# Gathered products of a sparse graph layer: units of 256 rows with 64-row quarters, paired half tiles, and the identity term folded into the matrix

## The chip, the cores and the metric

The kernel runs on one core of a Trainium2 chip. The time is the device time of that core in microseconds, the median of several executions. A profile is one execution taken by the hardware profiler; it has a span of its own, from the first to the last instruction.

## The reference

One layer of a graph network with a residual and a normalisation, in float32, for a batch of 8, 4096 nodes and 256 features:

```python
HW = einsum('bnf,fo->bno', x, W)
A_norm = relu((A + A.T) * 0.5)
D = sum(A_norm, axis=1);  d = where(D > 0, D, 1) ** -0.5
L_norm = eye(N) - d[:, None] * A_norm * d[None, :]
out = relu(einsum('nm,bmo->bno', L_norm, HW))
return layernorm(x + out, axis=-1, eps=1e-5)
```

A is 4096 x 4096 and mostly zero: an entry (i, j) is present with a probability that falls with i and j, so the first rows and columns are the densest; the diagonal is always present. After symmetrising, 70,020 of 16.8 million entries are not zero (counted from the inputs of seed 0).

With e = 1/d² and g = d · HW, an output row is relu(d (e g_self − Σ A_norm g)). This is the form that the kernel computes. The dense matrix is never multiplied: for each block of output rows the kernel lists the nodes with an entry in those columns of A, gathers their rows of g and their pieces of A from device memory, and multiplies tiles of 128 gathered rows.

## The kernel before

**Stage 1** goes through A in blocks of 512 x 512 (`NS` = 8 per side). For a pair (i, j), i ≤ j, SP's queue loads both blocks (`load_adj`, L201), and `symmetrise` transposes one on PE against the identity (L212), DVE adds the other (L215), ACT applies relu and the factor 0.5 (L216), DVE sums each row over the 128-wide column blocks into `part` (L217), and ACT's queue stores the block to `a_dram` (L223). When a row i of blocks is done, `degrees` sums `part`, sets `e` (L233) and lets POOL raise it to −0.5 for `r` (L234). Between the blocks `form` makes g, 128 nodes at a time: load x (SP, L241), transpose it on PE (L247), copy to SBUF on ACT (L248), multiply by W (L257), and scale by r on ACT (L266) into `g_dram`; the last 8 blocks are formed unscaled first, held in SBUF (L268), and scaled when r is known (`release`, L276). `a_dram` and `g_dram` have one row more, N, which holds zeros.

**Lists.** For four blocks of 128 output columns at once, `places` marks in `mask` which nodes have a positive sum in a block, counts them with two matmuls (triangular and all-ones matrices, L114, L115), and turns the running count into a place (tile, row) for each node (L117 to L143). `make_list` spreads the places of one block into one-hot matrices on DVE (`hot`, L149; `inn`, L156; `val`, L163 and L166), and 32 small bf16 matmuls collect the node numbers (L169). From these DVE makes the row numbers of g and of A (`gi`, `ai`, L183, L185). A place that nobody takes gets N, the row of zeros. `CAP` gives the number of tiles of each of the 32 blocks, 29 for the first, 9 for the last nine, 390 in all. Lists are made four blocks ahead; the order of instructions on an engine is that of a scheduler's planning, so some of them run in stage 1.

**Gathered products.** For block i, `gather` issues two indirect DMAs on POOL for each tile t: 128 pieces of A of 128 columns (`ga`, L358, 64 KB) and 128 rows of g of 2048 columns (`gg`, L365, 1 MB), each into one of 10 buffers. The product of a tile is four matmul calls (L384), one for each 512 columns (8 batches x 256 features are G = 2048), which add into four PSUM banks `py`; six banks are there for them. `finish` loads x again (`xr`, L313, SP's queue) and the block's own rows of g (`gself`, L394), lets DVE compute e·gself − py (L317), ACT relu with scale r (L325), and DVE the residual sum (L326), the moments (L331 to L333) and, after POOL's power (L334), the normalisation (L336). ACT's queue stores the result (L344).

After it stands a branch for the case that a list is too long (`over`); it forms the dense product and isn't entered for these inputs.

Of the kernel before, what the change touches and what calls it, by code (L numbers as in the profile page):

```python
# [16 lines left out]
CAP = [29, 21, 18, 17, 16, 15, 14, 13, 13, 13, 12, 12, 12, 11, 11, 11, 11] + [10] * 6 + [9] * 9  # L17


@with_exitstack  # L20
def kernel(
# [20 lines left out]

    nc = tc.nc
    B, N, F = x.shape
    FO = w.shape[1]
    P = 128
# [5 lines left out]
    G = B * FO  # L52
    HOLD = 8
    EPS = 1e-5

    const = ctx.enter_context(tc.tile_pool(name="const", bufs=1))
    dram = ctx.enter_context(tc.tile_pool(name="dram", bufs=1, space=bass.MemoryType.DRAM))
    psum = ctx.enter_context(tc.tile_pool(name="psum", bufs=6, space=bass.MemoryType.PSUM))
# [5 lines left out]
    part = const.tile([P, NB, NB], F32, name="part")  # L64
# [3 lines left out]
    r = const.tile([P, NB], F32, name="r")  # L68

# [11 lines left out]
    tmax = max(CAP)  # L81
# [19 lines left out]
    carry = const.tile([P, A, NB], F32, name="carry")  # L101
    nc.vector.memset(carry, 1.0)
    nc.vector.memset(carry[:, :, 0:1], 0.0)
    over = const.tile([P, NB], F32, name="over")

    def places(s):

        mask = ipool.tile([P, A, NB], BF16, tag="mask", name=f"mask_{s}")
        nc.vector.tensor_scalar(
            mask, part[:, :, s * A : (s + 1) * A].rearrange("p m i -> p i m"), 0.0, None, ALU.is_gt  # L110
        )
        pc = psum.tile([P, 2, A * NB], F32, tag="ix", name=f"count_{s}", bufs=2)
        mflat = mask.rearrange("p i m -> p (i m)")
        nc.tensor.matmul(pc[:, 0, :], lhsT=lower, rhs=mflat, start=True, stop=True)  # L114
        nc.tensor.matmul(pc[:, 1, :], lhsT=ones, rhs=mflat, start=True, stop=True)  # L115
        incl = ipool.tile([P, A * NB], F32, tag="incl", name=f"incl_{s}")
        nc.vector.tensor_tensor_scan(  # L117
            incl, carry.rearrange("p i m -> p (i m)"), pc[:, 1, :], 0.0, ALU.mult, ALU.add
        )
        for k in range(A):  # L120
            i = s * A + k
            nc.vector.tensor_scalar(
                over[:, i : i + 1],
                incl[:, (k + 1) * NB - 1 : (k + 1) * NB],
                float(CAP[i] * P),
                None,
                ALU.is_gt,
            )
        pos = ipool.tile([P, A * NB], F32, tag="pos", name=f"pos_{s}")
        nc.vector.tensor_sub(pos, incl, pc[:, 1, :])  # L130
        nc.vector.tensor_add(pos, pos, pc[:, 0, :])
        ip = ipool.tile([P, A * NB], I32, tag="ip", name=f"ip_{s}")
        nc.vector.tensor_copy(ip, pos)
        quot = ipool.tile([P, A * NB], I32, tag="quot", name=f"quot_{s}")
        nc.vector.tensor_single_scalar(quot, ip, 7, ALU.arith_shift_right)
        rem = ipool.tile([P, A * NB], I32, tag="rem", name=f"rem_{s}")
        nc.vector.tensor_single_scalar(rem, ip, P - 1, ALU.bitwise_and)

        at = ipool.tile([P, 2, A, NB], F32, tag="at", name=f"at_{s}")
        aq = at[:, 0].rearrange("p i m -> p (i m)")  # L140
        nc.vector.scalar_tensor_tensor(aq, quot, 1.0, mflat, ALU.add, ALU.mult)
        nc.vector.tensor_scalar(aq, aq, -1.0, None, ALU.add)
        nc.vector.tensor_copy(at[:, 1].rearrange("p i m -> p (i m)"), rem)  # L143
        return at

    def make_list(i, at):
        k, t = i % A, CAP[i]
        hot = ipool.tile([P, NB, P], BF16, tag="hot", name=f"hot_{i}")
# [3 lines left out]
            at[:, 1, k, :].unsqueeze(2).to_broadcast([P, NB, P]),  # L152
            ALU.is_equal,
        )
        inn = ipool.tile([P, NB, tmax], F32, tag="inn", name=f"inn_{i}", bufs=1)
# [3 lines left out]
            at[:, 0, k, :].unsqueeze(2).to_broadcast([P, NB, t]),  # L159
            ALU.is_equal,  # L160
        )
        val = ipool.tile([P, NB, 2, tmax], BF16, tag="val", name=f"val_{i}")
# [4 lines left out]
        pl = psum.tile([P, 2, tmax], F32, tag="ix", name=f"pl_{i}", bufs=2)  # L167
        for m in range(NB):
            nc.tensor.matmul(  # L169
                pl[:, :, :t],  # L170
                lhsT=hot[:, m, :],
                rhs=val[:, m, :, :t],
                start=(m == 0),
                stop=(m == NB - 1),
            )

        low = ipool.tile([P, tmax], F32, tag="low", name=f"low_{i}")
        nc.vector.tensor_copy(low[:, :t], pl[:, 1, :t])
        nc.vector.scalar_tensor_tensor(
            low[:, :t], pl[:, 0, :t], float(P), low[:, :t], ALU.mult, ALU.add  # L180
        )
        gi = ipool.tile([P, tmax], U32, tag="gi", name=f"gi_{i}", bufs=6)
        nc.vector.tensor_scalar(gi[:, :t], low[:, :t], float(N), None, ALU.add)  # L183
        ai = ipool.tile([P, tmax], U32, tag="ai", name=f"ai_{i}", bufs=6)
        nc.vector.tensor_scalar(  # L185
            ai[:, :t], low[:, :t], float(NB), float(N * NB + i), ALU.mult, ALU.add
        )
        lists[i] = (gi, ai)


    with (
# [4 lines left out]
        tc.tile_pool(name="stat1", bufs=2) as stat1,  # L196
    ):
# [9 lines left out]
        def symmetrise(i, j, tij, tji):  # L207
            sym = spool.tile([P, A, S], F32, tag="sym", name=f"sym_{i}_{j}")
            for a in range(A):
# [8 lines left out]
                part[:, i * A : (i + 1) * A, j * A : (j + 1) * A],  # L218
                sym.rearrange("p a (c q) -> p a c q", q=P),
# [5 lines left out]
            )  # L225

        def degrees(i):
            ms = slice(i * A, (i + 1) * A)
            deg = stat1.tile([P, A], F32, tag="deg", name=f"deg_{i}")
            none = stat1.tile([P, A], F32, tag="none", name=f"none_{i}")  # L230
            nc.vector.tensor_reduce(deg, part[:, ms, :], AX.X, ALU.add)
            nc.vector.tensor_scalar(none, deg, 0.0, None, ALU.is_le)
            nc.vector.tensor_add(e[:, ms], deg, none)  # L233
            nc.gpsimd.tensor_tensor(r[:, ms], e[:, ms], neg_half[:, :A], ALU.pow)  # L234

# [46 lines left out]
        for i in range(NS):  # L282
            for j in range(i, NS):
# [14 lines left out]
            known += range(i * A, min((i + 1) * A, NB - HOLD))  # L298
        for m in sorted(held):
            release(m)  # L300
        ats = {}
        ahead = 4
        for i in range(ahead):
            if i % A == 0:
                ats[i // A] = places(i // A)
            make_list(i, ats[i // A])
# [4 lines left out]
    def finish(i, gself, py, ypool, stat):  # L311
        xr = ypool.tile([P, B, F], F32, tag="xr", name=f"xr_{i}")
        nc.sync.dma_start(xr, x[:, i * P : (i + 1) * P, :].rearrange("b p f -> p b f"))  # L313
        y = ypool.tile([P, B, FO], F32, tag="y", name=f"y_{i}")
        yf = y.rearrange("p b o -> p (b o)")
        for c in range(G // S):
            nc.vector.scalar_tensor_tensor(  # L317
                yf[:, c * S : (c + 1) * S],
                gself[:, c * S : (c + 1) * S],
                e[:, i : i + 1],  # L320
                py[c],
                ALU.mult,
                ALU.subtract,
            )
        nc.scalar.activation(yf, yf, AF.Relu, scale=r[:, i : i + 1])  # L325
# [4 lines left out]
        for b in range(B):  # L330
            nc.vector.bn_stats(stats[:, b, :], y[:, b, :])  # L331
            nc.vector.bn_aggr(mv[:, b, :], stats[:, b, :])
        nc.vector.tensor_scalar(rstd, mv[:, :, 1], EPS, None, ALU.add)  # L333
        nc.gpsimd.tensor_tensor(rstd, rstd, neg_half[:, :B], ALU.pow)  # L334
# [9 lines left out]
        nc.scalar.dma_start(out[:, i * P : (i + 1) * P, :].rearrange("b p f -> p b f"), y)  # L344

    a_rows = a_dram.rearrange("j (c q) -> (j c) q", q=P)
    with (
        tc.tile_pool(name="gath", bufs=10) as gath,
        tc.tile_pool(name="ypool", bufs=2) as ypool,
        tc.tile_pool(name="stat", bufs=3) as stat,  # L350
    ):
        got = {}

        def gather(i):
            gi, ai = lists.pop(i)
            for t in range(CAP[i]):
                at = gath.tile([P, P], F32, tag="a", name=f"ga_{i}_{t}")
                nc.gpsimd.indirect_dma_start(  # L358
                    out=at,
                    out_offset=None,  # L360
                    in_=a_rows,
                    in_offset=bass.IndirectOffsetOnAxis(ap=ai[:, t : t + 1], axis=0),
                )
                gt = gath.tile([P, G], F32, tag="g", name=f"gg_{i}_{t}")
                nc.gpsimd.indirect_dma_start(  # L365
                    out=gt,
                    out_offset=None,
                    in_=g_dram,
                    in_offset=bass.IndirectOffsetOnAxis(ap=gi[:, t : t + 1], axis=0),
                )  # L370
                got[i, t] = (at, gt)

        gather(0)
        for i in range(NB):
            if i + ahead < NB:
                k = i + ahead
                if k % A == 0:
                    ats[k // A] = places(k // A)
                make_list(k, ats[k // A])
# [77 lines left out]
```

## Time and profile before

| | |
|---|---|
| median of 3 runs | 1980.01 us (1978.75 to 1981.48) |
| the profiled execution | 1980.13 us, span 1978.2 us |
| granted TensorE clock, mean | 0.969 of full speed |
| moved by DMA | 738 MB in the span, 373 GB/s |
| busy share of the span | PE 92%, DVE 45%, ACT 18%, POOL 46% |

Times in a profile are microseconds from the span's start, unless marked ns. PE is TensorE's matmuls, PEld its weight loads (they run beside matmuls), DVE VectorE, ACT ScalarE, POOL GpSimd, SP SyncE; a q behind the name is the engine's sequencer, which issues DMAs. In a group of instructions stand the line, engine, operation, output <- inputs, shapes and count; then the busy time in us and the mean of one in ns; then the idle time of the engine ahead of them and what ended it. The rows of busy tenths cut the span into 40 equal slices, a digit being the busy share in tenths. A queue's row gives packets, MB and the time that its packets took as a share of 16 DMA engines' span. The chain of waits follows the work that ended last back from the end: start, length, what. A list of waits gives the total in us, the times, and the longest.

### The profile page before, as it was taken

How to read it: one execution, taken by the hardware profiler on the slowest of the kernel's cores; microseconds unless marked ns; L12 is line 12 of the kernel's file. 1: busy time of each engine (PE TensorE's matmuls, PEld its weight loads, DVE VectorE, ACT ScalarE, POOL GpSimd, SP SyncE). 2: the span in 40 equal slices, each digit the busy share in tenths (PEclk: the TensorE clock that was granted, in tenths of full speed). 3: DMA queues.
4: the chain of work that ended last, by engine and by line, in shares of the span. 5: the costliest groups of instructions: out<-in, count | busy, mean ns of one | idle time of the engine just before them, and what ended most of it. 6: DMA issues, size and time to landing. Idle time of an engine off the chain costs nothing.

```text
span 1978.2 us, 18260 instructions
## 1 busy us (share of the span) xinstructions
PE 1819.9 (92%) x6720; PEld 1006.8 (51%) x6720; DVE 887.4 (45%) x1679; ACT 348.1 (18%) x361; POOL 918.9 (46%) x830
## 2 busy tenths in 40 slices
PE   6988686879669999999999999999999999999995
PEld 5877575768544444444444444444444444444442
DVE  4778898755300102432226424523733733343334
ACT  3654443545620000000000000000000000000000
POOL 0000000000045655676558766865766865666662
PEclk8999897899889999999999999999999999999998
DMA  9998999999979999999998999899899999999994
GB/s 345 384 372 328 349 369 337 353 397 382 400 278 409 387 357 369 342 378 380 381 383 317 411 409 389 338 411 413 313 401 411 368 407 411 410 412 412 413 410 191
DMA packets 245726, 738.08 MB, mean 373 GB/s; under 512 B 17136, under 2 KB 115744, under 8 KB 187520
## 3 DMA queue, kind: packets, MB, share of 16 engines
q0 software_dynamic: 68640, 434.55, 55.3%
q1 hardware_dynamic: 104960, 167.78, 23.8%
q10 hardware_dynamic: 72032, 134.51, 17.7%
q8 instruction: 56, 0.92, 0.2%
q14 instruction: 38, 0.31, 0.0%
HBM read 602.54 MB, written 134.24 MB: 372 GB/s over the span
## 4 chain that ended last, share of the span: by engine, by line
PE 68%; DMA 13%; DVE 11%; issue 4%; ACT 3%; POOL 1%; SPq 0%; ACTq 0%; POOLq 0%; DVEq 0%
PE py L384 54%; PE pg L257 8%; DMA gg<-g_dram,gi 7%; PE tr L212 3%; DVE hot L149 3%; DMA a_dram<-sym 2%; DVE sym L215 2%; DMA adj<-in_adj_dram 2%; PE xtr L247 2%; DVE part L217 1%; ACT sym L216 1%; DMA xin<-in_x_dram 1%; PE pl L169 1%; DVE stats L331 1%; DVE y L326 1%
## 5 line engine op out<-in xcount | busy, mean ns | idle before, releaser
L384 PE MATMUL py<-gg,ga 128*128 128x512 f32 x3120 | 1363.6, 596 | 18.4 <-issue 16.0
L384 PEld LDWEIGHTS py<-gg,ga 128*128 128x128 f32 x3120 | 585.7, 190 | 726.6 <-issue 717.7
L358 POOL DMA_INDIRECT ga<-a_dram,ai x390 | 425.0, 1090 | 269.8 <-PE py L384 145.2
L365 POOL DMA_INDIRECT gg<-g_dram,gi x390 | 414.9, 1064 | 226.4 <-DMA gg<-g_dram,gi 109.7
L325 ACT ACTIVATE y<-y,r 128x2048 f32<-128x2048 f32 x32 | 64.1, 2002 | 1332.8 <-DVE y L317 1213.5
L257 PE MATMUL pg<-w_sb,xt 128*128 128x256 f32 x1024 | 247.6, 398 | 38.2 <-ACT xt L248 38.1
L317 DVE SCALAR_TENSOR_TENSOR y<-gself,e,py 128x512 f32<-128x512 f32 x128 | 95.1, 747 | 408.0 <-PE py L384 398.6
L234 POOL TENSOR_TENSOR r<-e,neg_half 128x4 f32<-128x4 f32 x8 | 8.1, 1011 | 510.3 <-DVE e L233 510.3
L257 PEld LDWEIGHTS pg<-w_sb,xt 128*128 128x128 f32 x1024 | 198.9, 199 | 76.3 <-ACT xt L248 48.5
L215 DVE TENSOR_TENSOR sym<-tr,adj 128x512 f32<-128x512 f32 x256 | 158.3, 683 | 115.4 <-PE tr L212 105.3
L212 PE MATMUL tr<-ident,adj 128*128 128x128 f32 x1024 | 132.1, 289 | 58.5 <-DVE sym L215 34.6
L185 DVE TENSOR_SCALAR ai<-low 128x9 uint32<-128x9 f32 (+11 forms) x32 | 6.5, 204 | 369.1 <-DMA ga<-a_dram,ai 369.1
L149 DVE TENSOR_TENSOR hot<-iota_q,at 128x4096 bf16<-128x4096 f32 x32 | 141.4, 4420 | 63.9 <-PE pl L169 48.9
L212 PEld LDWEIGHTS tr<-ident,adj 128*128 128x128 f32 x1024 | 123.7, 150 | 65.9 <-DVE sym L215 40.3
L217 DVE TENSOR_REDUCE part<-sym 128x16 f32<-128x2048 f32 x64 | 144.7, 2278 | 13.1 <-ACT sym L216 13.1
L216 ACT ACTIVATE sym<-sym 128x2048 f32<-128x2048 f32 x64 | 122.5, 1914 | 111.2 <-DVE sym L215 110.6
L336 DVE TENSOR_SCALAR y<-y,mv,rstd 128x256 f32<-128x256 f32 x256 | 87.2, 412 | 43.4 <-POOL rstd L334 43.4
L331 DVE BATCH_NORM_STATS2 stats<-y 128x6 f32<-128x256 f32 x256 | 99.3, 400 | 0.9
L326 DVE TENSOR_TENSOR y<-y,xr 128x2048 f32<-128x2048 f32 x32 | 73.4, 2293 | 56.0 <-ACT y L325 45.7
L334 POOL TENSOR_TENSOR rstd<-rstd,neg_half 128x8 f32<-128x8 f32 x32 | 69.5, 2173 | 42.2 <-DVE rstd L333 41.6
L248 ACT COPY xt<-xtr 128x512 f32<-128x512 f32 x128 | 69.8, 582 | 62.1 <-PE xtr L247 50.9
L247 PE MATMUL xtr<-ident,xin 128*128 128x128 f32 x512 | 72.5, 297 | 7.6 <-DVE sym L215 7.2
(50 smaller groups left out, 398.4 us busy)
## 6 DMA issues: line engine op xcount, KB each, us to landing
adj<-in_adj_dram SPq DMA_DIRECT2D x64, 1024.0 KB
a_dram<-sym ACTq DMA_DIRECT2D x64, 1024.0 KB
xin<-in_x_dram SPq DMA_DIRECT2D x32, 1024.0 KB
gself<-g_dram SPq DMA_DIRECT2D x32, 1024.0 KB
xr<-in_x_dram SPq DMA_DIRECT2D x32, 1024.0 KB
out_dram<-y ACTq DMA_DIRECT2D x32, 1024.0 KB
g_dram<-gt ACTq DMA_DIRECT2D x24, 1024.0 KB
g_dram<-held ACTq DMA_DIRECT2D x8, 1024.0 KB
```

Source lines behind the costliest of these rows:

```text
L149: nc.vector.tensor_tensor(hot, iota_q.unsqueeze(1).to_broadcast([P, NB, P]), at[:, 1, k, :].unsqueeze(2).to_broadcast([P, NB, P]), ALU.is_ ...
L212: nc.tensor.transpose(pt[:, c * P : (c + 1) * P], tji[:, c, a * P : (a + 1) * P], ident)
L215: nc.vector.tensor_add(sym[:, a, :], pt, tij[:, a, :])
L216: nc.scalar.activation(sym, sym, AF.Relu, scale=0.5)
L217: nc.vector.tensor_reduce(part[:, i * A : (i + 1) * A, j * A : (j + 1) * A], sym.rearrange("p a (c q) -> p a c q", q=P), AX.X, ALU.add,)
L247: nc.tensor.transpose(pt[:, k, c, :], xin[:, b + k, c * P : (c + 1) * P], ident)
L257: nc.tensor.matmul(pg[:, k * FO : (k + 1) * FO], lhsT=xt[:, b + k, c, :], rhs=w_sb[:, c, :], start=(c == 0), stop=(c == FC - 1),)
L317: nc.vector.scalar_tensor_tensor(yf[:, c * S : (c + 1) * S], gself[:, c * S : (c + 1) * S], e[:, i : i + 1], py[c], ALU.mult, ALU.subtract,)
L331: nc.vector.bn_stats(stats[:, b, :], y[:, b, :])
L358: nc.gpsimd.indirect_dma_start(out=at, out_offset=None, in_=a_rows, in_offset=bass.IndirectOffsetOnAxis(ap=ai[:, t : t + 1], axis=0),)
L365: nc.gpsimd.indirect_dma_start(out=gt, out_offset=None, in_=g_dram, in_offset=bass.IndirectOffsetOnAxis(ap=gi[:, t : t + 1], axis=0),)
L384: nc.tensor.matmul(py[c], lhsT=at, rhs=gt[:, c * S : (c + 1) * S], start=(t == 0), stop=(t == CAP[i] - 1),)
```

## The change

Output rows are taken in 16 **units** of 256 instead of 32 blocks of 128. A unit has four quarters of 64 rows; `part` now sums A by 64 columns. `patterns` gives each node a number of four bits, which quarters of the unit use it (the node's own quarter is always marked). Nodes of a pattern share tiles: kind 1 is the first quarter alone, 3 the first two, 12 the last two, 6 the middle two, and so on (`KINDS`); kind 0 takes what is left, patterns with three or four quarters and what didn't fit, and is multiplied for all 256 rows. `CAPS` gives the tiles of each kind, 317 in all.

Of a tile only the quarters that its kind names are multiplied (`targets`). A kind with one quarter of a block needs 64 of the 128 columns of the stationary operand; `steps_of` puts such tiles together, 1 with 2, 4 with 8, 5 with 10, and the two blocks' halves of 6 and 9, so that calls for the lower and the upper 64 output rows alternate. Kinds 0, 6, 9, 5 and 10 gather 256 columns of A (1 KB a row), the others 128.

Each gathered row of g serves the whole unit. The gathers of g check bounds: an index of N is skipped and nothing is moved. The rows so left alone hold old finite data and meet zeros in A; therefore the 13 buffers of g, a ring of fixed places, are cleared once.

The term e·g_self goes into A: `degrees` subtracts e from the diagonal of the 128 x 128 diagonal blocks and stores these again, so that the product is Σ A_norm g − e g_self; ACT then evicts each bank with relu and scale −r, and `gself`, its load and DVE's pass go.

Lists are made in steps spread over the loops (counts, places of the fitting, places of the rest, one-hots, collecting), up to four units ahead; in the product stage their matmuls write to two of the four banks of a unit's first block. Each of the two blocks of a unit has four banks. x for the residual is loaded two blocks ahead on ACT's queue, the result is stored by SP's, and `after` puts the moments, the normalisation and the lists off by one, five and two steps.

The core of the diff:

```diff
-CAP = [29, 21, 18, 17, 16, 15, 14, 13, 13, 13, 12, 12, 12, 11, 11, 11, 11] + [10] * 6 + [9] * 9
+KINDS = [1, 2, 3, 0, 6, 9, 5, 10, 12, 4, 8]
+CAPS = [
+    [5, 2, 4, 12, 1, 2, 3, 1, 1, 1, 1],
+    [4, 3, 2, 6, 1, 1, 1, 1, 1, 3, 3],
+    [4, 3, 1, 4, 1, 1, 1, 1, 1, 3, 3],
...
+    [3, 3, 1, 3, 0, 0, 0, 0, 0, 3, 3],
+]
...
+            if i == j:
+                for a in range(A):
+                    nc.gpsimd.tensor_copy(diag[:, a, :], sym[:, a, a * P : (a + 1) * P])
...
+            nc.vector.tensor_scalar(minus_r[:, ms], r[:, ms], -1.0, None, ALU.mult)
+            nc.vector.tensor_scalar(minus_e, e[:, ms], -1.0, None, ALU.mult)
+            for a in range(A):
+                m = i * A + a
+                nc.vector.scalar_tensor_tensor(
+                    diag[:, a, :], ident, minus_e[:, a : a + 1], diag[:, a, :], ALU.mult, ALU.add
+                )
+                nc.scalar.dma_start(
+                    a_dram[m * P : (m + 1) * P, m * P : (m + 1) * P], diag[:, a, :]
+                )
...
+    def evict(i, py, ypool):
+        y = ypool.tile([P, B, FO], F32, tag="y", name=f"y_{i}", bufs=3)
         for c in range(G // S):
-            nc.vector.scalar_tensor_tensor(
+            nc.scalar.activation(
+                y.rearrange("p b o -> p (b o)")[:, c * S : (c + 1) * S],
                 py[c],
+                AF.Relu,
+                scale=minus_r[:, i : i + 1],
+            )
...
+    def steps_of(u):
+        of = {k: list(range(f, f + c)) for k, f, c in zip(KINDS, first[u], CAPS[u])}
+        out = []
+        for one, two in ((1, 2), (3, None), (0, None), (6, None), (9, None), (5, 10), (12, None), (4, 8)):
+            a, b = of[one], of.get(two, [])
+            for n in range(max(len(a), len(b))):
+                out.append([(k, ts[n]) for k, ts in ((one, a), (two, b)) if n < len(ts)])
+        return out
...
+            gt = ring[n % RING]
+            nc.gpsimd.indirect_dma_start(
+                out=gt,
+                out_offset=None,
+                in_=g_dram,
+                in_offset=bass.IndirectOffsetOnAxis(ap=gi[:, t : t + 1], axis=0),
+                bounds_check=N - 1,
+                oob_is_err=False,
+            )
...
+        def lists(u):
+            one = psum.tile([P, S], F32, tag="b0", name=f"lists0_{u}")
+            two = psum.tile([P, S], F32, tag="b0", name=f"lists1_{u}")
...
+            if u + 4 < NU:
+                count(u + 4, tot, low)
+            if u + 3 < NU:
+                count_rest(u + 3, pr[:, 0], pr[:, 1])
+            if u + 2 < NU:
+                collect(u + 2, pl)
+                index(u + 2, pl)
+            if u + 3 < NU:
+                place_rest(u + 3, pr[:, 0], pr[:, 1])
+            if u + 4 < NU:
+                place(u + 4, tot, low)
...
+            work = [(b, rows, *got[u, t]) for m in range(2) for k, t in step for b, rows in targets(k)[m : m + 1]]
...
+            for c in range(G // S):
+                for (b, rows, at, gt), new_rows in zip(work, fresh):
+                    both = any(len(targets(k)) == 2 for k, t in step)
+                    off = b * P if both else 0
                     nc.tensor.matmul(
-                        py[c],
-                        lhsT=at,
+                        py[2 * u + b][c][rows, :],
+                        lhsT=at[:, off + rows.start : off + rows.stop],
                         rhs=gt[:, c * S : (c + 1) * S],
```

More of the change, by code (lines that the diff above doesn't have):

```diff
@@ new lines @@
+    for k in range(NK):
+        nc.gpsimd.memset(kinds[:, k : k + 1], float(KINDS[k] or -1))
+        for u in range(NU):
+            nc.gpsimd.memset(limit[:, u, k : k + 1], float(CAPS[u][k] * P))
+            nc.gpsimd.memset(base[:, u, k : k + 1], float(first[u][k] * P + 1))
+    own = const.tile([P, QU, 2], F32, name="own")
+    nc.vector.memset(own, 0.0)
+    for s in range(QU):
+        h = slice((s % 2) * Q, (s % 2 + 1) * Q)
+        nc.vector.memset(own[h, s, s // 2 : s // 2 + 1], 1.0)
@@ L115, in places @@
[L115 to L118, printed above, removed]
-        )
[L120 to L148, printed above, removed]
+        diag = used[:, :, 2 * u : 2 * u + 2]
@@ L149, in make_list, with spread @@
+    def spread(u):
+        at, t = plan[u], tiles[u]
+        hot = ipool.tile([P, NB, P], BF16, tag="hot", name=f"hot_{u}", bufs=1)
         nc.vector.tensor_tensor(
@@ L349 @@
         tc.tile_pool(name="ypool", bufs=2) as ypool,
         tc.tile_pool(name="stat", bufs=3) as stat,
+        tc.tile_pool(name="psum2", bufs=4, space=bass.MemoryType.PSUM) as psum,
     ):
-        got = {}
[L354 to L379, printed above, removed]
-            py = [psum.tile([P, S], F32, tag="ps", name=f"py_{i}_{c}") for c in range(G // S)]
-            for t in range(CAP[i]):
-                at, gt = got.pop((i, t))
-                for c in range(G // S):
+        ring = [gath.tile([P, G], F32, tag=f"g{k}", name=f"g{k}", bufs=1) for k in range(RING)]
@@ new lines, with gather @@
+        for gt in ring:
+            nc.vector.memset(gt, 0.0)
+        steps = [(u, step) for u in range(NU) for step in steps_of(u)]
+        order = [(u, k, t) for u, step in steps for k, t in step]
+        got = {}
+        def gather(n):
+            if n >= len(order):
+                return
+            u, kind, t = order[n]
+            gi, ai = plan[u]
+            both = len(targets(kind)) == 2
+            at = gath.tile([P, 2 * P], F32, tag="a", name=f"ga_{u}_{t}")
+            nc.gpsimd.indirect_dma_start(
+                out=at if both else at[:, :P],
+                out_offset=None,
+                in_=a_pairs if both else a_rows,
+                in_offset=bass.IndirectOffsetOnAxis(ap=ai[:, t : t + 1], axis=0),
+            )
+            gt = ring[n % RING]
+            nc.gpsimd.indirect_dma_start(
+                out=gt,
+                out_offset=None,
+                in_=g_dram,
+                in_offset=bass.IndirectOffsetOnAxis(ap=gi[:, t : t + 1], axis=0),
+                bounds_check=N - 1,
+                oob_is_err=False,
+            )
+            got[u, t] = (at, gt)
@@ new lines, with after, finish, rest @@
+        later = []
+        def after(n, fn, *args):
+            later.append((n, fn, args))
+        for n in range(RING):
+            gather(n)
+        n = RING
+        xr = {i: residual(i, ypool) for i in range(2)}
+        py = {}
+        left = {}
+        def finish(i):
+            y = evict(i, py.pop(i), ypool)
+            def rest():
+                mv, rstd = moments(i, y, xr.pop(i), stat)
+                if i + 2 < NB:
+                    xr[i + 2] = residual(i + 2, ypool)
+                after(5, normalise, i, y, mv, rstd)
+            after(1, rest)
@@ L394 @@
-            nc.sync.dma_start(gself, g_dram[i * P : (i + 1) * P, :])
-            finish(i, gself, py, ypool, stat)
+                        start=new_rows,
+                        stop=left[b] == 0,
+                        skip_group_check=True,
+                    )
+            for k, t in step:
+                gather(n)
+                n += 1
+            for b in {wk[0] for wk in work}:
+                if left[b] == 0:
+                    finish(2 * u + b)
+                    if b == 0:
+                        after(2, lists, u)
```

258 lines of the change are left out of this document (200 added, 58 removed), and 12 rows, old and new, of the table CAPS.

## The prediction, made before the result was known

> **What bounds the kernel now.** I read the busy shares and slices first, then the busy times of four stages, then the chain of waits, then the queues.
>
> ```profile
> span 1978.2 us, 18260 instructions
> PE   6988686879669999999999999999999999999995
> DMA  9998999999979999999998999899899999999994
> L384 PE MATMUL py<-gg,ga 128*128 128x512 f32 x3120 | 1363.6, 596 | 18.4 <-issue 16.0
> L384 PEld LDWEIGHTS py<-gg,ga 128*128 128x128 f32 x3120 | 585.7, 190 | 726.6 <-issue 717.7
> ```
>
> ```profile
> 0.00:562.50 562.50, 449.19 (x2886) 395.58 (x2886) 385.49 (x469) 282.76 (x327) 19.22 (x28) 0.92 0.97 359
> 562.50:578.50 16.00, 0.02 (x1) 0.05 (x1) 0.00 (x0) 1.30 (x3) 7.62 (x8) 0.64 0.72 275
> 578.50:1957.50 1379.00, 1370.38 (x3834) 611.14 (x3834) 492.50 (x1183) 62.05 (x31) 890.43 (x793) 1.00 0.99 385
> 1957.50:1978.20 20.70, 0.28 (x1) 0.00 (x0) 9.42 (x28) 2.00 (x1) 1.63 (x1) 0.64 0.15 52
> ```
>
> The second fence is the busy time by stage: length, PE, weight loads, DVE, ACT, POOL (instructions in brackets), granted clock, DMA share, GB/s. Stage 1 (symmetrising A, forming g) takes 562.5 us, a gap 16, the gathered products 1379, the tail 20.7. The change aims at the third. There PE and the DMA engines are both full: PE busy 1370 of 1379, DMA share 0.99 at 385 GB/s. A bound that falls only on one of them buys nothing.
>
> ```profile
> 716.59 37.86 PE py L384 x88
> 765.81 51.61 PE py L384 x120
> PE py L384 <- DMA gg<-g_dram,gi: 2.4, 2, 1.4
> POOL ga L358 <- PE py L384: 145.2, 140, 2.9
> ```
>
> In the chain a matmul record starts every 51.61/120 = 0.430 us. 390 tiles x 4 column chunks are 1560 calls but 3120 records, so each fp32 call is two passes; a tile costs 8 x 0.430 = **3.44 us**, all tiles 1342 of the 1379, and about 37 go to the lists' matmuls and small gaps. PE waits 2.4 us for gathered rows; POOL waits 145 for PE to free tiles. PE is the bound by a hair.
>
> **PE after the change.** From CAPS and the grouping in steps_of: 317 tiles instead of 390. In units of 3.44 us: 141 full products (kinds 3 and 12 one each, the 60 tiles of kind 0 two each), 134 pairs of half products (1 with 2, 4 with 8, both halves of 6 and 9, two pairs from 5 with 10), 12 halves without a partner. Calls rise: (141 + 268 + 12) x 8 = 3368 records against 3120. So everything hangs on what a pair costs. No row of before shows two matmuls in different columns of the array at once. From below a pair costs one slot, since each half still streams 512 columns; from above two. The nearest rows: weight loads of 190 ns run inside the 430 ns spacing without lengthening it, and records last 596 ns at 430 ns spacing, so the engine already holds two matmuls in different phases. I take one slot: (141 + 134 + 12) x 3.44 = **987 us**; the upper end is 3368 x 0.430 = 1448.
>
> The Trainium skill, TensorE: Matmul & The Clock Gate, Part 3, gives 2.38x for three column tiles side by side; an estimate from it is 1.13 slots a pair, 60 us more than my sum. The same part says that a weight load overlaps matmuls in flight only where the row group differs, which speaks against this change (rival 2). In the rows above, loads that use all 128 rows are hidden behind matmuls that use all 128 rows, so for full tiles the trace disagrees.
>
> Switching between half and full tiles happens up to four times a unit (after 1/2, before 6, around 12). If each lets the array run empty it costs what the overlap hides, 596 - 430 = 0.17 us: 64 x 0.17 = 11. It could be nothing; I take 11. Lists: 14 of 16 now fall in this stage, each 32 small matmuls; before, 22 fell there (3834 - 3120 records, less the counts, by 32) within the 37 us, 1.7 each, so 24, plus some 10 for the wider counts. PE in all 987 + 34 + 11 = **1032 us**.
>
> **DMA after the change.** Counted from the reference's inputs (seed 0): the 16 units use 35,513 gathered rows of g in all. Before, 390 x 128 = 49,920 rows were moved, padding included. After, the bounds check leaves padding out: 35,513 x 8192 B = 291 MB against 409. A: 213 tiles of 64 KB and 104 of 128 KB, 27.6 MB against 25.6. gself (33.6 MB) goes, since e stands in A's diagonal; xr and out stay, 67. Sum 386 MB against 535. At the stage's 385 GB/s: **1002 us**.
>
> ```profile
> q0 software_dynamic: 68640, 434.55, 55.3%
> q1 hardware_dynamic: 104960, 167.78, 23.8%
> q10 hardware_dynamic: 72032, 134.51, 17.7%
> ```
>
> The queues check this: gathers took 0.553 x 1978.2 = 1094 us for 434.55 MB, 2.52 us/MB; the two others 2.8 and 2.6. 318.5 x 2.52 + 67 x 2.7 = 983.
>
> So PE 1032, DMA 1002, but not in the same units. Unit 0 has 44 slots, 151 us and 3 for its share of the 45, for 3849 rows and 39 MB, 102 us of DMA; units 1 and 2 lean to PE as well; later it is mostly the other way: unit 15 has 13 slots, 45 + 3 us, against 1699 rows and 19.4 MB, 50. Thirteen ring buffers carry less than one late unit over. The sum of the larger of both, over the 16 units, comes to **1068**.
>
> **POOL, ACT, DVE in the stage.**
>
> ```profile
> 549.86 0.95 POOL L358 DMA_INDIRECT ga<-a_dram,ai  x1 [0.30 <-issue]
> 551.12 0.96 POOL L358 DMA_INDIRECT ga<-a_dram,ai  x1 [0.30 <-issue]
> L334 POOL TENSOR_TENSOR rstd<-rstd,neg_half 128x8 f32<-128x8 f32 x32 | 69.5, 2173 | 42.2 <-DVE rstd L333 41.6
> L266 ACT ACTIVATE gt<-pg,r 128x512 f32<-128x512 f32 x96 | 64.9, 690 | 75.4 <-PE pg L257 73.3 <-issue 2.1
> L317 DVE SCALAR_TENSOR_TENSOR y<-gself,e,py 128x512 f32<-128x512 f32 x128 | 95.1, 747 | 408.0 <-PE py L384 398.6
> L326 DVE TENSOR_TENSOR y<-y,xr 128x2048 f32<-128x2048 f32 x32 | 73.4, 2293 | 56.0 <-ACT y L325 45.7
> L331 DVE BATCH_NORM_STATS2 stats<-y 128x6 f32<-128x256 f32 x256 | 99.3, 400 | 0.9
> L332 DVE BATCH_NORM_AGGREGATE mv<-stats 128x2 f32<-128x6 f32 x256 | 41.5, 167 | 0.0
> POOL gg L365 <- DMA gg<-g_dram,gi: 109.7, 96, 3.1
> ```
>
> POOL issues back to back every 1.26 us: 634 gathers are 799, with 32 rstd at 2.2 us 869 of 1068. Hidden, but with little slack (its waits for earlier gathers to land, 110 now, come on top where they remain), and in order: a gather behind an rstd waits for DVE's moments, which `after` puts off by five steps. The bounds check's own issue cost has no row; between nothing and doubling the 0.96 us (+304). I take nothing, as the descriptors are one per row as now.
>
> Eviction moves from DVE (4 x 0.747) to ACT (4 x 0.690), which had 62 us of work in 1379; hidden. The wait added on PE is the banks': `lists` borrows two of b0's four banks between b0's end and the next unit, and DVE must read them before the third chunk of the next unit starts. Ahead on DVE stands the add of 2.29 and the statistics (8 x 0.40 and 8 x 0.17 in this stage), some 7 us; b1's last three or four slots give 10 to 14 us. Bounds nothing to 5 us a unit, 0 to 70; behind that matmul everything on PE waits. Late units have slack of some 3 us, so I take 10 in all. Stage: 1068 + 10 = **1078**.
>
> **Stage 1, gap and tail.**
>
> ```profile
> 500.00:550.00 50.00, 34.85 (x176) 30.45 (x177) 10.00 (x13) 35.54 (x39) 4.28 (x5) 0.86 0.98 380
> L141 DVE SCALAR_TENSOR_TENSOR at<-quot,mask 128x128 f32<-128x128 int32 x8 | 2.3, 285 | 0.0
> L234 POOL TENSOR_TENSOR r<-e,neg_half 128x4 f32<-128x4 f32 x8 | 8.1, 1011 | 510.3 <-DVE e L233 510.3
> L223 ACTq DMA_DIRECT2D a_dram<-sym x64: 366/366/441, 16.8 to 516.3; - x64
> 481.41 10.76 DMA a_dram<-sym
> L149 DVE TENSOR_TENSOR hot<-iota_q,at 128x4096 bf16<-128x4096 f32 x12 | 53.0, 4419 | 0.0
> L217 DVE TENSOR_REDUCE part<-sym x64: 2273/2276/2287, 18.3 to 516.3; 128x16 f32<-128x2048 f32 x64
> 568.43 0.96 POOL L365 DMA_INDIRECT gg<-g_dram,gi  x1 [8.78 <-DMA g_dram<-gt]
> 562.45 16.02 issue
> ```
>
> Each of eight `degrees` gains minus_r (behind POOL's 1.01 us), minus_e, four diagonal products at 0.285 and four DMA issues on ACT at 0.366: DVE 8 x 3 = 24 us, ACT 8 x 1.5 = 12. The reduction reads the same 2048 elements: nothing. 32 diagonal copies go to POOL, which does 19 us in 562; its price is open (0 to 1.01 each), and hidden. DVE loses ten lists: 12 `hot` ran in stage 1 at 4.42, with about 2 of smaller steps each; now two spreads and the new patterns and places, some 45 against 77; this pays for the 24. The DMA share of 0.97 sets stage 1's pace; 2 MB more is 6 us. The last row's diagonal write must wait for the block (7,7) it overwrites, a landing like the 10.76 above, on ACT, which paces the end (35.5 of 50). Behind it the held tiles' scaling queues. Bounds 0 to 25; I take 10. The 13 ring clears lie between nothing and a pass over 2048 elements, 2.28 each, 30 in all; DVE is 40 of 50 us idle there: hidden. The gap's causes, g's last landing and the first gathers, stay: 16. Tail 20.7.
>
> Sum: 578.5 + 10 + 1078 + 20.7 = 1687 of span, plus the 1.9 by which the profiled run's time (1980.13) exceeds its span: **1689 us**. That run is 0.1 us from the median of 1980.01.
>
> **Rivals.**
> 1. *No overlap* (the other side): half products follow each other. PE 1448 + 34 + 11 = 1493; 578.5 + 10 + 1493 + 22.6 = 2104. It decides from 1.73 slots a pair on: 526 us of full and single slots plus 461 times that, plus 45, fill the 1369 that would give 1980. For it: no row shows overlap, and nothing now excludes strictly successive matmuls. Chance 0.15.
> 2. *Weight loads uncovered in half-tile steps.* Two halves x two passes x four chunks x 134 pairs = 2144 loads, each between 95 ns (half of 190) and 190: 204 to 407 more on PE, so 1236 to 1439 there and 1847 to 2050 in all; by the lower end, the load in proportion to its columns, 1847. Against it: loads are covered now. This is what the row-group rule of the Trainium skill's Part 3, named above, would make of the change. Chance 0.10.
> 3. *POOL or the banks set the pace.* A gather of g at 0.3 to 0.5 us more gives POOL 960 to 1030 and unhidden waits; bank stalls of 5 us a unit add 70: 1720 to 1800. For it: POOL's small slack. Chance 0.10.
> 4. *Padding is moved after all*: 40,576 rows, 41 MB more, 108 us of DMA, partly under PE in early units: 1780. Chance 0.03.
>
> **Chances.** The forecast, a pair within 1.15 slots, 0.62: from 1603 (DMA's 1002 and nothing added) to 1760. The range 1610 to 1900 holds the forecast, rivals 3 and 4 and half of 2, about 0.8. Faster by over 0.2% (what a measurement here can tell) 0.83, within 0.01, slower 0.16.
>
> **What would show it.** In chains within half-tile steps, records counted in pairs should give 0.43 us a pair, not 0.86; loads that end a wait there would show rival 2. DMA in the stage should carry about 386 MB, the gather queue 318. Early units should show POOL waiting for PE, late ones PE waiting for gathers. POOL without waits but always busy is rival 3. Stage 1 should end near 590. The forecast is wrong if a pair costs over 1.15 slots, or if neither PE nor DMA is above 0.9 in the stage.

## The result, and the profile after

The changed kernel takes **1779.5 us** (median of 4 runs, 1776.2 to 1783.7) against 1980.7 (4 runs) for the kernel before: ratio 0.898, 95% interval [0.896, 0.901]. It is 10% faster, within the range and in the direction forecast, but 90 us above the predicted 1689.

From the page of the changed kernel, the span, the busy tenths of PE and DMA in 40 slices, and two groups:

```profile
span 1778.2 us, 18495 instructions
PE   6998686868866799999999999998979849679874
DMA  9999999999977984797999999899998986877973
L623 PE MATMUL py<-g,ga 128*64 128x512 f32 (+1 forms) x3368 | 1058.3, 601 | 108.8 <-ACT y L449 82.4
L449 ACT ACTIVATE y<-py,minus_r 128x512 f32<-128x512 f32 x128 | 83.5, 688 | 1104.9 <-PE py L623 639.9
```

Before, the PE row was nines to its end. Now holes stand in its last third, and in the DMA row at or beside the same places: neither of the two resources that the forecast weighed is the bound there. Busy times by stage say when it begins (length, then PE, weight loads, DVE, ACT, POOL with instruction counts, granted clock, DMA share, GB/s; the four stretches after the gap are unit 0, units 1 to 4, 5 to 10, 11 to 15, each up to the start of its last unit's last eviction):

```profile
0.00:571.40 571.40, 446.97 (x2638) 388.19 (x2638) 381.02 (x546) 284.46 (x328) 42.58 (x427) 0.91 0.96 357
571.40:587.00 15.60, 0.00 (x0) 0.00 (x0) 8.72 (x5) 0.69 (x1) 9.17 (x10) 0.56 0.84 307
587.00:743.10 156.10, 156.06 (x417) 62.06 (x418) 5.72 (x18) 4.81 (x7) 67.47 (x68) 0.99 0.72 273
743.10:1037.70 294.60, 294.60 (x1165) 114.59 (x1164) 123.09 (x369) 21.93 (x33) 214.70 (x182) 1.00 0.95 362
1037.70:1465.40 427.70, 378.16 (x1451) 141.00 (x1450) 186.24 (x542) 30.58 (x49) 314.43 (x263) 0.95 0.94 352
1465.40:1759.80 294.40, 245.58 (x836) 98.33 (x834) 109.26 (x336) 25.52 (x42) 154.52 (x131) 0.91 0.74 271
1757.50:1778.20 20.70, 0.00 (x0) 0.00 (x0) 10.97 (x34) 2.42 (x4) 2.26 (x2) 0.59 0.44 149
```

The forecast had the first product at 588.5 (it is 587.0), unit 0 at 154 us (156.1), units 1 to 4, by the larger of PE and DMA in each, at 301 (294.6), the tail at 20.7 (20.7). Units 5 to 15 were to take 613 and take 722. The whole error is there, and in the last stretch the DMA share is 0.74: the engines that move data wait too.

The list of waits of the changed kernel (total us, times, longest) names the wait:

```profile
ACT y L449 <- DMA out_dram<-y: 438.2, 15, 43.1
PE py L623 <- ACT y L449: 82.4, 7, 23.6
PE py L623 <- DMA g<-g_dram,gi: 10.6, 7, 4.2
```

ACT's evictions wait for **a store of the output to land**, and PE waits for ACT. The chain of waits shows one turn of it (start, length, what):

```profile
1290.50 4.33 DVE hot L244
1294.84 2.60 DVE y L472 x8
1297.49 18.99 DMA out_dram<-y
1317.32 42.51 PE py L623 x110
```

An eviction writes a tile y, which then takes the residual, is normalised in place (L472) and stored. There are three such tiles. Block i can be evicted only when block i - 3 has been stored; until then its four banks are full, and PE, which needs them for the next unit, stands. The normalisation comes five steps after the moments, here also behind a list's 4.33 us on DVE, and then the store takes 19 us to land:

```profile
L480 SPq DMA_DIRECT2D out_dram<-y x32: 372/372/387, 778.6 to 1771.1; - x32
DMA to landing us min/median/max: 5.1/18.8/25.1
```

In the long early units there is time for this. In late ones, where a unit is to last 50 us, it is not enough: three stored blocks are one and a half units.

### The profile page after: what moved, and what is told of

The parts are those of the page before. It is cut to its first block, busy times and chain, and to the rows that moved or that the text cites. A ratio compares the mean times of both kernels' runs of the same rounds, so it can differ in the third digit from the quotient of the medians.

```text
span 1778.2 us, 18495 instructions
## 1 busy us (share of the span) xinstructions
PE 1521.4 (86%) x6504; PEld 804.2 (45%) x6504; DVE 823.4 (46%) x1841; ACT 368.7 (21%) x457; POOL 804.5 (45%) x1079
## 3 DMA queue, kind: packets, MB, share of 16 engines
q0 software_dynamic: 57456, 318.57, 46.5%
q10 hardware_dynamic: 76640, 136.61, 20.7%
## 4 chain that ended last, share of the span: by engine, by line
PE 54%; DMA 19%; issue 12%; DVE 9%; ACT 3%; POOL 2%; ACTq 0%; POOLq 0%; SPq 0%; DVEq 0%
PE py L623 43%; DMA out_dram<-y 7%; PE pg L374 6%; DMA g<-g_dram,gi 5%; DMA adj<-in_adj_dram 5%; PE tr L315 3%; DVE sym L318 2%; DVE y L472 1%; DVE g L514 1%; ACT sym L319 1%; DVE part L320 1%; ACT xt L365 1%; POOL g L536 1%; POOL ga L527 1%; PE xtr L364 1%
## 5 line engine op out<-in xcount | busy, mean ns | idle before, releaser
L623 PE MATMUL py<-g,ga 128*64 128x512 f32 (+1 forms) x3368 | 1058.3, 601 | 108.8 <-ACT y L449 82.4
L623 PEld LDWEIGHTS py<-g,ga 128*64 128x64 f32 (+1 forms) x3368 | 400.7, 157 | 754.0 <-issue 647.4
L536 POOL DMA_INDIRECT g<-g_dram,gi x317 | 385.2, 1215 | 295.3 <-PE py L623 176.2
L527 POOL DMA_INDIRECT ga<-a_dram,ai x317 | 336.2, 1060 | 131.4 <-issue 84.9
L449 ACT ACTIVATE y<-py,minus_r 128x512 f32<-128x512 f32 x128 | 83.5, 688 | 1104.9 <-PE py L623 639.9
L320 DVE TENSOR_REDUCE part<-sym 128x32 f32<-128x2048 f32 x64 | 144.2, 2277 | 19.6 <-ACT sym L319 19.6
L472 DVE TENSOR_SCALAR y<-y,mv,rstd 128x256 f32<-128x256 f32 x256 | 86.9, 412 | 89.3 <-POOL rstd L470 89.3
L383 ACT ACTIVATE gt<-pg,r 128x512 f32<-128x512 f32 x96 | 66.0, 690 | 99.7 <-PE pg L374 77.4
L470 POOL TENSOR_TENSOR rstd<-rstd,neg_half 128x8 f32<-128x8 f32 x32 | 53.5, 1673 | 48.0 <-DVE rstd L466 47.3
L244 DVE TENSOR_TENSOR hot<-iota_q,at 128x4096 bf16<-128x4096 f32 x16 | 70.6, 4415 | 0.0
L364 PEld LDWEIGHTS xtr<-ident,xin 128*128 128x128 f32 x512 | 59.9, 146 | 13.1 <-ACT gt L383 6.8
## 6 DMA issues: line engine op xcount, KB each, us to landing
out_dram<-y SPq DMA_DIRECT2D x32, 1024.0 KB, 18.8
```

The costliest lines, as they stand in the source:

```text
L320: nc.vector.tensor_reduce(part[:, i * A : (i + 1) * A, j * S // Q : (j + 1) * S // Q], sym.rearrange("p a (c q) -> p a c q", q=Q), AX.X, A ...
L364: nc.tensor.transpose(pt[:, k, c, :], xin[:, b + k, c * P : (c + 1) * P], ident)
L472: nc.vector.tensor_scalar(y[:, b, :], y[:, b, :], mv[:, b, 0:1], rstd[:, b : b + 1], ALU.subtract, ALU.mult,)
L527: nc.gpsimd.indirect_dma_start(out=at if both else at[:, :P], out_offset=None, in_=a_pairs if both else a_rows, in_offset=bass.IndirectOff ...
L536: nc.gpsimd.indirect_dma_start(out=gt, out_offset=None, in_=g_dram, in_offset=bass.IndirectOffsetOnAxis(ap=gi[:, t : t + 1], axis=0), boun ...
L623: nc.tensor.matmul(py[2 * u + b][c][rows, :], lhsT=at[:, off + rows.start : off + rows.stop], rhs=gt[:, c * S : (c + 1) * S], start=new_ro ...
```

## The experiments

I had one theory for the missing 90 us, called O (output buffers), and rivals: D, the transfers run slower than forecast; P, POOL's order. The side-by-side halves and the skipped padding, on which the sum rested, were to be tested by themselves, and then stage 1's end, where two terms seemed to cancel.

**e1: a fourth buffer for y.**

```diff
-        y = ypool.tile([P, B, FO], F32, tag="y", name=f"y_{i}", bufs=3)
+        y = ypool.tile([P, B, FO], F32, tag="y", name=f"y_{i}", bufs=4)
-        tc.tile_pool(name="gath", bufs=RING + 2) as gath,
+        tc.tile_pool(name="gath", bufs=RING) as gath,
-        stats = stat.tile([P, B, 6], F32, tag="stats", name=f"stats_{i}")
+        stats = stat.tile([P, B, 6], F32, tag="stats", name=f"stats_{i}", bufs=2)
```

> One more buffer for y, four instead of three; to make room, the A tiles get 13 buffers instead of 15 and the statistics 2 instead of 3. Theory O (output buffers): in the changed kernel evictions wait 438 us on ACT for an earlier block's store, and PE waits 82 for ACT; with a fourth buffer a block has a whole block's time more, so PE's wait for ACT falls under 20 and the time to 1690-1725. Rival D (the transfers): the late units are paced by a DMA rate under 385 GB/s, the wait for the store only shows who is last; then PE waits for gathers instead and the time stays within 15 of 1779.

Measured: 1711.0 us, ratio to before 0.865 [0.863, 0.867]. The waits of e1:

```profile
ACT y L449 <- DMA out_dram<-y: 84.1, 3, 33.5
PE py L623 <- DMA g<-g_dram,gi: 9.2, 6, 3.3
```

ACT's wait for stores falls from 438 to 84 us, PE's wait for ACT is no longer in the list, and 68 of the 90 us are gone. O holds; D as the main cause does not.

**e2: the normalisation two steps behind instead of five**, three buffers as in the changed kernel.

```diff
-                after(5, normalise, i, y, mv, rstd)
+                after(2, normalise, i, y, mv, rstd)
```

> The normalisation two steps behind the moments' issue instead of five; three buffers as in the changed kernel. Theory O: each store starts some three steps, about 10 us, sooner and its buffer comes free as much sooner, so 30 to 60 us of the 82 go: 1720-1750. Rival P (POOL's order): the power that belongs to it now stands in POOL's queue before DVE has the moments ready, gathers behind it wait, and the time is equal or longer, 1780-1830. Rival D: no change beyond 10.

Measured: 1726.1 us, ratio 0.872 [0.868, 0.875]. Its waits:

```profile
ACT y L449 <- DMA out_dram<-y: 168.1, 6, 33.2
PE py L623 <- ACT y L449: 10.1, 1, 10.1
```

The same wait shrinks by another way, with no memory added; P's price doesn't appear.

**e3: the calls of a step in serial order.**

```diff
-            for c in range(G // S):
-                for (b, rows, at, gt), new_rows in zip(work, fresh):
+            for (b, rows, at, gt), new_rows in zip(work, fresh):
+                for c in range(G // S):
```

> Only the order of the matmul calls in a step is changed: all four column chunks of one half tile, then all four of the other, so that calls for the same 64 output rows follow each other. Theory S (side by side): the gain comes from two halves in the array at once; this order lets only the seam overlap, a pair costs nearly two slots of 3.44 us, 134 x 3.44 = 461 us more on PE less what the late units have spare: 2060-2150. Rival: halves overlap or are short whatever the order; then within 20 of 1779.

Measured: 1830 us (2 runs, ratio 0.925 [0.917, 0.932]). Both expectations missed.

**e5: no half products**; the same passes, rows and transfers, all 128 columns.

```diff
-                out.append((b, {1: slice(0, Q), 2: slice(Q, P), 3: slice(0, P)}[h]))
+                out.append((b, slice(0, P)))
```

> The changed kernel with every half product made a full one: the same 3368 matmul passes on the same rows, with all 128 columns of A as the stationary operand (the added columns are zeros). If the gain on PE comes from two half products in the array at once, all 421 products take a slot of 0.430 x 8 us: 1448 + 45 on PE, the whole 587 + 1493 + 23 = about 2100, at least 2060. If passes were limited elsewhere, or halves had not run side by side in the changed kernel either, within 30 of 1779. Between them the serial order of e3 has 1830.

Measured: 2073 us (2 runs), ratio 1.046 [1.043, 1.049], slower than before the change. Unit 1 is bound by PE in all three and has 10 pairs, 15 full products and one single half. Its window, from its first product to the first of unit 2, for the product's matmuls alone (length; PE and weight loads busy, with the records; clock; DMA share; GB/s), in the changed kernel, then e3, then e5:

```profile
744.23:835.65 91.42, 90.22 (x288) 34.96 (x290) 1.00 0.86 323
```

```profile
754.42:854.49 100.07, 98.09 (x288) 39.36 (x290) 1.00 0.81 298
```

```profile
770.50:895.90 125.40, 124.19 (x289) 54.63 (x290) 1.00 0.68 244
```

In e5 the 36 products take 36 x 3.44 = 123.8 and 1.6 is left, of which the lists' matmuls, which stand between the products, take 1.3. In the changed kernel 26 slots are 89.4, and 2.0 is left, for the lists and up to four switches between half and full tiles (forecast: 2.1 and 0.7). So a pair of halves costs **one slot** of 3.44 us and two full products cost two.

Stretches of one sort inside the unit show it without the lists. In the changed kernel these are three pairs and the single half, then 14 full products, then four pairs; the last row is the same four pairs in e3:

```profile
744.24:758.11 13.87, 13.87 (x56) 4.40 (x56) 1.00 1.02 405
758.11:806.37 48.26, 48.26 (x113) 21.20 (x112) 1.00 0.89 336
806.38:820.26 13.88, 13.88 (x65) 4.51 (x64) 1.00 0.71 242
```

```profile
818.66:836.31 17.65, 17.65 (x65) 6.42 (x64) 1.00 0.56 189
```

Four pairs take 13.88 us, 0.434 for two records: what the forecast had asked to see (0.43, not 0.86). Three pairs and a single half take as long, so the half alone costs a whole slot: halves are not shorter, two of them run side by side. In e3 the four pairs take 17.65, 1.28 slots each, and the whole unit with its ten pairs takes 8.7 us more than in the changed kernel, 1.25 slots a pair. Halves for different output rows overlap even where the four calls (eight passes) of one half stand before the other's in program order. Why the engine can, these runs don't settle. I had taken the order for the cause; it is the half-width tiles, and the order is worth a quarter of it.

**e4: padding gathered again.**

```diff
-                bounds_check=N - 1,
-                oob_is_err=False,
```

> The gathers of g without the bounds check: padding fetches the row of zeros again, 40,576 rows instead of 35,513, 41 MB more. If the skipped rows are really not moved now, the gather queue carries 360 MB instead of 319 and late units get longer: 108 us at 385 GB/s, less what hides in unit 0 (about 9 MB) and in waits for y's buffers: 1820-1880. If the check's price at issue on POOL paces late units, 1750-1780.

Measured: 1862.5 us (2 runs, ratio 0.941 [0.938, 0.944]), 83 more than the changed kernel. The gather queue (packets, MB, share of 16 engines' span) in the changed kernel, then e4:

```profile
q0 software_dynamic: 57456, 318.57, 46.5%
```

```profile
q0 software_dynamic: 57456, 360.03, 49.4%
```

The difference is 41.5 MB, the 5063 padding rows: skipped rows move nothing, though the number of packets is the same. 108 us of DMA at 385 GB/s became 83. Part of it can hide where PE paces, but the 83 are not transfers alone: PE's wait for ACT's evictions grew as well, from 82.4 to 124.9 us. The two were not separated.

**e6: e1 and e2 together; e8: five buffers and a ring of 12.** What is left once y's buffers are enough?

```diff
-    RING = 13
+    RING = 12
-        y = ypool.tile([P, B, FO], F32, tag="y", name=f"y_{i}", bufs=3)
+        y = ypool.tile([P, B, FO], F32, tag="y", name=f"y_{i}", bufs=5)
```

(e8; its A tiles are 12, its statistics 2.)

> Four buffers for y (as in e1) and the normalisation two steps behind (as in e2). Theory O: the buffers' wait was cut by each alone; together nothing of it is left, and the stage is at its floor of transfers and passes: 1695-1712, no more than 15 below e1's 1711. If the early normalisation has a price of its own on POOL, 1712-1730.

> Five buffers for y, paid for with one buffer of the ring (12 instead of 13) and 12 for A. Theory O says that the fourth buffer took nearly all of the wait: 1700-1715, ACT waiting under 30 us for stores (84 in e1). If buffers for y still set the pace after the fourth: 1670-1695. If the ring's depth matters more: 1715-1740.

Measured: e6 1704.5 (ratio 0.859 [0.856, 0.861]), e8 1703.2 (0.860 [0.858, 0.862]). Both are 7 to 8 us under e1, and in neither list of waits does a store of the output stand any more. Four buffers and an earlier normalisation, or five buffers, are the end of this.

**e7: the diagonal blocks stored by POOL's queue**, on top of e1; **e9: the same on the changed kernel**, with three buffers.

```diff
-                nc.scalar.dma_start(
+                nc.gpsimd.dma_start(
                     a_dram[m * P : (m + 1) * P, m * P : (m + 1) * P], diag[:, a, :]
```

> As e1, with the 32 stores of A's diagonal blocks issued by POOL's queue instead of ACT's. In the changed kernel ACT waits 7.1 us for block (7,7) to land before it may issue the last ones, with the held tiles' scaling behind it, and stage 1 ends 9 us later than before the change. If that wait and the 12 us of issues are the cause: 6 to 10 us less than e1, 1701-1706, and the first gathered product at about 579 instead of 587. If the transfers pace stage 1, or POOL's own issue is dearer: within 3 of e1.

> The changed kernel with one thing changed: the diagonal blocks are stored by POOL's queue, not ACT's; three buffers for y. e7 had the first product 22 to 26 us sooner than the changed kernel and e1. If ACT's queue is the cause, with the held tiles waiting behind block (7,7), the start moves from 587 to 563-568 here too and the time to 1750-1763. If e7's gain needed the fourth buffer, within 8 of 1779.

Measured: e7 1687.9 us (ratio 0.853 [0.850, 0.856]), 23 under e1; e9 1761.2 (0.891 [0.887, 0.895]), 18 under the changed kernel, the first product at 564.7 us. The edit gains by itself, and in e7 more than twice what I gave it. The timeline shows how. The changed kernel:

```profile
515.01 8.86 PE L374 MATMUL pg<-w_sb,xt 128*128 128x256 f32 x32 [1.94 <-ACT xt L365]
...
525.48 0.81 ACTq L349 DMA_DIRECT2D a_dram<-diag  x2
526.33 0.69 ACT L383 ACTIVATE gt<-pg,r 128x512 f32<-128x512 f32 x1 [7.12 <-DMA a_dram<-sym]
544.38 9.68 PE L374 MATMUL pg<-w_sb,xt 128*128 128x256 f32 x32 [16.65 <-ACT xt L365]
```

and e7:

```profile
502.35 8.86 PE L374 MATMUL pg<-w_sb,xt 128*128 128x256 f32 x32 [1.94 <-ACT xt L365]
...
512.85 2.21 POOL L349 DMA_DIRECT2D a_dram<-diag  x4 [6.73 <-DMA a_dram<-sym]
523.45 8.64 PE L374 MATMUL pg<-w_sb,xt 128*128 128x256 f32 x32 [10.50 <-ACT xt L365]
```

In brackets stands the idle time and its end. On ACT the wait of 7.12 us for block (7,7) holds the scaling of the held tiles and the copies for the last three blocks of g; PE's wait for them is 16.65. On POOL the wait is about as long and nobody stands behind it: PE's wait is 10.5, as before the change, and the step that follows starts 21 us sooner. The formation step ahead of that one starts 12.7 us sooner already (502.35 in e7, 515.01 in the changed kernel), so the last wait is worth some 8. The rest is most likely the diagonal stores of earlier rows on ACT, which were not moved one by one. At the fourth row of blocks, in the changed kernel, four of them hold ACT's queue for 8.61 us, and ACT stands idle for 13.33:

```profile
376.98 8.61 ACTq L349 DMA_DIRECT2D a_dram<-diag  x4
385.64 1.91 ACT L319 ACTIVATE sym<-sym 128x2048 f32<-128x2048 f32 x1 [13.33 <-DMA a_dram<-sym]
```

The windows of e7 (from the first product on, in the stretches used above):

```profile
565.10:720.80 155.70, 155.70 (x418) 61.93 (x419) 5.71 (x18) 4.83 (x8) 67.47 (x68) 0.98 0.73 274
720.80:1015.30 294.50, 294.50 (x1165) 115.03 (x1164) 122.29 (x369) 21.97 (x32) 216.46 (x185) 1.00 0.95 364
1015.30:1389.60 374.30, 358.47 (x1406) 134.54 (x1405) 180.66 (x530) 31.68 (x49) 281.19 (x231) 0.99 0.95 355
1389.60:1659.90 270.30, 261.78 (x882) 102.47 (x882) 107.83 (x321) 26.59 (x41) 187.54 (x162) 0.98 0.94 352
```

**e10 and e11: the edits together**, e6 and e8 with POOL's queue for the diagonal.

> e7 and the normalisation two steps behind. e6 stood 6 us under e1, in the noise of both; if the stage is at its floor of transfers and passes, 1675-1690. If the order on POOL has a price, above 1695.

> e8 (five buffers for y, a ring of 12) with the diagonal blocks stored by POOL's queue. The two gains should add: e8's 1703 less 22 is 1681; 1674-1690.

Measured: e10 **1680.6 us** (1678.9 to 1685.1), ratio 0.850 [0.848, 0.852]; e11 1682.4, ratio 0.849 [0.847, 0.852]. They add, and both beat the changed kernel by some 98 us. In e10's list of waits no store of the output stands; what PE still waits for is gathers:

```profile
PE py L623 <- DMA g<-g_dram,gi: 20.6, 18, 2.4
```

## Why the prediction was right or wrong

**The cost of a pair: right.** "I take one slot" decided the sign, and unit 1 gives it twice, by 91.4 us against the 92.2 that the forecast's terms give for it, and by e5's 125.4. Rival 1, with 2104 for products that don't overlap, is what e5 built: 2073. So it was no idle rival; without overlap the change loses 4.6%.

**Rival 2 (weight loads uncovered) did not happen.** The changed kernel's loads by shape:

```profile
L623 PEld LDWEIGHTS py<-g,ga 128*128 128x128 f32 x1128 | 217.3, 195 | 372.5 <-issue 279.3 <-ACT y L449 88.2 <-DMA ga<-a_dram,ai 4.8
L623 PEld LDWEIGHTS py<-g,ga 128*64 128x64 f32 x2240 | 183.5, 137 | 381.5 <-issue 368.2 <-DMA ga<-a_dram,ai 8.9 <-DMA g<-g_dram,gi 1.0
```

A half's load takes 137 ns, between the bounds of 95 and 190; a pair needs four of them in 860 ns a chunk, and the pair still takes one slot, so they are hidden. The Trainium skill, TensorE: Matmul & The Clock Gate, Part 3, lists loads as overlapping matmuls in flight only where the row group differs; in the same part it also names loads into a background weight buffer, which the forecast left out. These halves share all 128 rows, and the measurement decides against the list's "only". The 2.38x that the same part of the Trainium skill gives for three column tiles, from which I had estimated 1.13 slots a pair, is not what two halves gave here: 1.0.

**Bytes: right, rate a little high.** The gather queue moved 318.57 MB, forecast 318.5. What the 33.6 MB of gself save by themselves was not run. In units 5 to 15, with the wait for y nearly gone, DMA gives 355 and 352 GB/s at a share of 0.95 and 0.94 (e7), not 385. These units take 645 us in e7 against the forecast's 613, most likely by this; what lowers the rate wasn't tried. Units 0 to 4 give 5 back, and the 10 us for the banks, which did not arise, another 10, so that e7's whole stage is 1095 against 1078.

**Eviction on ACT, called "hidden": the step that failed.** ACT's work was sized rightly (688 ns a bank against 690), but an engine's idle time is no proof that its instruction can start. I asked which bank and which engine the eviction needs and not which buffer it writes. In the kernel before, `finish` had two y tiles and a block lasted 31 us or more with the normalisation straight behind; here blocks end in twos, the normalisation is put off by five steps, and y has three tiles. "The wait added on PE is the banks'" named the wrong wait: no product of the changed kernel waits for the lists' readers on DVE, and in place of the 10 us for banks PE waits 82 for evictions that wait for y's stores. Some 70 us of the 90 are this, by e1, e2 and e6.

**Stage 1: the sum right by luck, two terms wrong.** The forecast was 10 later than before, and it was 8.5. But ACT's share was not 12 us of issues and a wait, hidden in part: e7 and e9 take 22 away with it. So something else pays 13: with ACT relieved the first product stands at 565, ahead of the old kernel's 578.5. I had let DVE's relief from ten lists only cancel DVE's additions; that it does more is the nearest reason, and wasn't tried.

**Rivals 3 and 4.** The measured 1779.5 lies in rival 3's range (1720 to 1800) and on rival 4's 1780, but neither is what happened. The issues on POOL (min/median/max ns, first and last start), the gathers of g in the changed kernel, then in e4, without the bounds check:

```profile
L536 POOL DMA_INDIRECT g<-g_dram,gi x317: 984/1003/6176, 577.2 to 1713.4; - x159
```

```profile
L536 POOL DMA_INDIRECT g<-g_dram,gi x317: 935/946/5213, 583.4 to 1792.9; - x159
```

The check takes 57 ns an issue, 18 us in all, not 0.3 to 0.5 us each; POOL is busy 751 of the four stretches' 1173 us. It set no pace. Padding is not moved (e4).

With the wait for y and ACT's queue mended, e10's 1680.6 is near the predicted 1689, but by errors that cancel: its first product stands at 565.0, 23 us before the forecast's 588.5, and its stage, to the end of the products at 1655, takes 1090 instead of 1078.

## What to carry to other kernels

When a stage gets shorter, count the life of every buffer in it, from its first write to the landing of its store, against the time that its number of copies now spans; an engine that is idle can still be the one that waits. Put a DMA that must wait for an earlier store's landing on a queue behind which nothing of the critical path stands. Where two limits are near each other, add them up unit by unit by the larger of the two: for units 0 to 4 that held to some 2%, for units 5 to 15, with the buffers mended, to 5%.

## What the runs showed of the hardware that I had not expected

Half products for different output rows overlap even with eight passes of one ahead of the other in program order (1.25 to 1.28 slots a pair in e3 against 1.0 alternating and 2.0 as full products). A weight load of 64 columns takes 137 ns against 195 for 128, so halving the columns doesn't halve it. A 1 MB store beside the gathers takes 18.8 us to land (median), against 10.0 for the 1 MB stores of A's blocks in stage 1 of the same kernel; the two also differ in queue and layout, so the cause is open.
